# A two-layer decoder on one Trainium2 core: tokens loaded a second time turned, the key layout on GpSimd, and the border between the layers written out by hand

## The chip, the cores and the metric

The kernel runs on one core of one Trainium2 chip. The metric is the device time of one execution in microseconds; a kernel's time is the median of its runs. One further execution is recorded by the profiler, and all views come from that one. The engines are TensorE (PE, with its weight loads as PEld), VectorE (DVE), ScalarE (ACT), GpSimd (POOL) and SyncE (SP), which only issues transfers. ACT and POOL can issue transfers too. Every engine works through its own queue of instructions strictly in order.

## The reference, cut to what matters

Sixteen sequences of 256 tokens with 128 features each go through two post-norm decoder layers. Everything is float32.

```python
# layer 0
x1 = ln(x + causal_self_attention(x, 16 heads of 8))
x2 = ln(x1 + cross_attention(x1, ctx, 8 heads of 16))      # ctx: 64 rows per sequence
g  = softmax(x2 @ gate_w.T)                                  # 64 experts, the best 6 per token,
y  = sum over 6 of g_e * w2_e @ (silu(w1_e x2) * (w3_e x2))  # 64 slots per expert
x3 = ln(x2 + y + shared_expert(x2))
# layer 1
x4 = ln(x3 + causal_self_attention(x3, 16 heads of 64))
x5 = ln(x4 + cross_attention(x4, ctx, 16 heads of 64))
out = ln(2 * x5 + width_limited_self_attention(ln(x5)))
```

## The kernel before, in words

The host lays out inputs (transposes only) and launches one program. Its work falls into three stages.

**Layer 0** (lines 654 to 925). The program `contexts` (768) and sixteen programs `layer0(b)` (798), one per sequence, are recorded engine by engine and then interleaved: the string `ORDER0` names, letter by letter, whose next unit on which engine comes next. So the order on PE, DVE, ACT and POOL is that of the string (`manual_schedule`), and SP's is the scheduler's. `layer0(b)` loads 256 tokens `x` (801), turns them on PE with an identity matrix and copies the result to `xT` on DVE (803), multiplies by the query and key weights into one PSUM bank `qk` (808), and takes from it the scaled queries `qT` on DVE (810) and the keys laid out four times, each masked to a quarter of the heads (`kx`, 812: `expanded`, two copies on DVE and two on ACT, each 128x256). Then come the values, the scores (`s_0a`), softmax (`nm_0a`, `p_0a`), the turned probabilities (`ptp_0a`, `pT_0a`), the outputs, cross attention (`kx0x` is its key layout, on POOL, 839), and the gate. The gate picks six experts per token (`chosen`), counts earlier tokens per expert with a running sum `run` (889 to 892, on DVE; the next sequence's `pos` matmul reads it), computes slots, and for each of twelve choices DVE computes `hit` (the weight) and POOL scatters the tokens into `xb` in memory by an indirect transfer (914). `clear_slots` (688) fills `xb` with zeros first, from SP's queue. The context program folds weights of layer 1's cross attention and writes `gd` and `hd` to memory.

**Experts** (lines 929 to 1074). The expert weights come in eight groups, four in flight. A shared expert (`shared_hidden`, `shared_out`) runs over all tokens in eight groups of 512: products `sh`, then `hs` on ACT and DVE, then the product `z`, which DVE adds to `x2`. The routed experts read `xb` (`xe`), turn it, compute `eh`, `he` and `yp`, and store `ye` to `yb`. Groups 4 to 7 of the shared expert come last.

**Layer 1** (lines 1076 to 1234). First two buffers `vaf` are zeroed on POOL (1088), and the value bias is carried through the output projection: `bv` on DVE, eight products `bv_out` on PE, added to `l1_bout` (1091 to 1097). Then sixteen programs `layer1(b)` (1099) are interleaved by `ORDER1`. Each gathers twelve rows per token pair from `yb` by indirect transfers on POOL (`ge`, 1107), combines them on DVE with the token's weights (`xr`, 1121), normalises, turns, and goes on with self attention (`qk1`, `s_1a`), `xpb_1a` on POOL (1157, which reads `l1_bout`), cross attention over `gx` and `hx` (loaded by SP from `gd` and `hd`) and the last attention. The stage is allotted memory when the experts' is given up, so SP's first `gx` load waits for the last `z` to have been computed. The experts' part, the bias and layer 1 are three separate hand-ordered stretches, and between them the scheduler may mix their instructions; the profile shows that it put batch 0's `xr` among the shared expert's last instructions on DVE.

A helper records every operation, so nearly all instructions of the profile have the line 141 (140 afterwards); they are told apart by the names of the tiles.

Of the kernel before, what the change touches and what calls it, by code (L numbers as in the profile page):

```python
# [34 lines left out]
    ',\'#\'#$#$+$(#)($()*#*))$(*)*)()*))*())*)()*(*()*#*$#*#$**($**(#*)#$%(\'\'$%()\'\')(()*()*(1*)0-#.*((*-**.-(*..(*)#*'  # L35
    '**(///%.(*-/%).(.#/)#/.+.)+/($)-\'/$%.(%\'\'-)\'-./(/./()/--.*#./)(/-)*65/($-*2#)/#/.3(-*$2%).3((442))*-33$43\'\'.4-'
    '-./-./-/.((*/-)(-/)#//+-$/)-\'/.(/2)//%\'3(34-)33*4-)2;:/4.43(-)224242)+4)7.#+3#%34#3+438404$2.0\'4-))27.4%3+8-92'
    '92.%3+8\'3-3-.22/))2+34.4-.+42/23/-47.4-842))+/4#.+4-$-.42\'./324-4-/74.9))%+89\'8+-829.98082.97)+@493-82?7.39-77'
    '.5/87359<9.29#9-.97#.03823908289237984=7$2.7.0433078748293979828497.7.038922937340$<9=79=22978<4932.9.03#9>7>0'
    '=$>%=\'>\'57<938..00=2=7>#382>#3:=#.4.08>730EA%%8<:%=B>$D=\'2\'37<<><><353>A8=7=5>=7>85><>=B9<A>873#9358>C#C%5=B97'  # L40
    'B$<C%<8\'\'=B$C7=<\'\'9<3>35<8=>77>8<85=<9=#>7>$79<>87>A3358>5>=>B:<BC<8#B>73#3>58BC$75<8C$\'9<A>8C%37\'85JAACACA8:='
    '#BBC:BCB<I=CF#CBC?AG=?C<88A%F=CG%:<HFH=#BG:G$<H%G\'\'<H=AA8>8:B=<=:A>ACAB>ABC<C=#CB8C8:<B>AC=<$C:<=\'A=>AC<<A>C=<'
    'BCFC=C%8:8\'GAGH:GGH?AF=CHB88:HG<:OAF=B<HNFF=>GDFGHK=H#HHBD<H=AHF%=?=BGAB?HGAL$?AB\'\'FKHGCFLFM=M=?BBA?CGFCGABHFF'
    'HGHAGC=HF=?BAGAHBFBC?LFHAHAKFLCHBKHGH==?HMLLMA?FBMKLDHLMBLAM=K=?BLAMBK?LLCFLMBMMFKHM=AB?TKMP#MSMKBDGMLFQKPGMDP'
    'LRQKIRKLGIQLFKBBDMGLFKGDLMFMLFGMKQHK$KMBFBDGMKHG#MDK$HFMG#MFLMK$HMPB\'BDMGR%QRD\'QFQFRKGGQHQRFBBFDK#HMRGLD$FK\'PG'
    'RLI%PG\'NPRBFBPRDGPLFQKDYGHLQKNRUGR#RX#LRQ%FGRK%KGPIGL#IQM#QRLIL%K%PMVM$KURG\'G\'ILUWWQKVIPMLPQVV$WV\'\'WQKKLPLMGPG'
    'RIQKRKPQMRPLIQKPRLPR#NRRLUGRGI$RQRIVKVPWPLKVR#LVM#GRGILWPIW$KLWPRU%GI_LQPVUQUNWUWVUWZVNVW#VSW[QSWWPLLUQW$NP$\'\''
    '%UZQW\'\'NV[P]][P^QUULRLNVQPQNURUWUVRUVWPWQZWVPLRLNWUQVPWPWQUQN[UR#WUWVPWP#RWLLNQWPUN]Q%%[S]QPUZQWLLNV[NdP[]U`Q#'
    'VcR[X]#Q]VXP%QU%QSQVZ[aS]$[\'U\'SZVZ[]U][]UV]ZZQQW`S[]VU]ZVSW]U[`WaZ]V]b[bUQZQWS[ZVaa$Sba\'\'b[UUVZVW[Z]U[]UZ[W]ZQ'
    'ZQSV]UZV]S#]]`X$]V][]QQSaUZVbZaSUa#]VaW#$]VbZbUQVSiZe]#bh#V%X[$%Z`[%\'\'Xf^a``[^b`baZb`[VZVXba#[baZXbabZ[b`$]`eb'  # L50
    '\'\'[%ZVgVeX[]#gXaZ]f`%#[a%Zf]`$[\'f\'VgVXfagZZ[`X[]a`b`abZabZ$]b`[\'\'Z`bVVX[`bebXb^ab`b[Zbf`V#bVX[fgZf#Xn[f]`$gm[`'
    'g#$Zbg[je%[^[a$`fe\'\'^eagege^fg#fgcfgac#g[[gf`#a^$g`k\'e%a^%\'`%`aejg[b[#^fkll`a%^eaeb$bf\'a\'e[[e^fgefgegf^`fg`kbe'
    'gaeg``gaea[b[^#g%`^$`ebfgj\'\'ag`kjgaglkcl[k^sealkrkl`keoag`lfaepjfblahjjljlfh`aejoaqcfqkeflckeklefloljkgklaaecf'
    'ljfgclekgpjjfkkegaajcfkelffeckjgkleplpejgljfejlaacfjlloclhlflkqepjfqjalaecpljfgpcpqfjloqkpqaacpeqfjcxooqowqokq'
    'thpmpqffhkqjqpoqkhpuqmjotkqffhpjuvvujhkotpoluvkkjolflofhpoqkqohqjppqjplkqoujqjqkokfoflhqjjohlqkjpqtqkqvmuofvfh'
    'kuuhvjoktuqvpvujoftkhplttvktrvvprjkokmpuopvmuovuvuvopvkqktmpopmtqvouqttpuuotqktkvmptuvoopvtpmutquvooqvtpvovptv'
    'kmktvuvmvvtrptovutpkokmupmqpwuwokkptmmutrutpprrtuvtuuvtpvprurtvuttuuvpprttrvutuwpprutrutuvuptprurwpurwuuwwuuuu'
    'uuwuuwwwwwww'
)
ORDER1 = (  # L60
    '&\'&$&$&&$&$$&$+,#$#+$)#%&#%+#$%$#$%)#%+#%#%#%$+$#%$$#$#)%+#$)#$$%)010$%$&.%+$#$&)%($&#)%$$(&%$%)+%($$&*$$&)#*('
    '%0.(*#*(%%0(%(*(*$$*)&(*))#&)*6)#)%0.(%#0($)#;.5*##%#$5%#$%(.%$$%($&$%)%&$%)&#$*)&3*#0))#+#.%#))%-+%.(%0%*53#*'
    '5(%#*)-$+$(/&-).*)+(/$-*)&#$*(5))#*))**$#*+$%+-/$%-&/$-/$&#/%$(5(*))..#*.(%.+.%$%+#$&)3-&$.#/:3#%-%3#/.5:-$-/3'
    '-.&8-/:($.)(&()*5($*(&*82*:)#)$*-)*)*3+*).+#)./($+/+..(%0(..*(*(0*2*3:#*$2/3(8/:-*..4480(0-.-/)-)&/-/2.3/2+..0'
    '/2)/..(042)/3(3/.30)44(4)*2)*#)4)-$/-$%2$%$2)%2%2.303/-34844:#.8#$#%$#%#$%2$$%73%-8%%%.--./-/-/#/.#.70%./.70/$'
    '8/-8/.09#.#/$0$#%#%#%-%--/-/#//#92%$3#3-4$+43+32+4335(43(&*5$2*(33\'@*5)*/5-)4+)32+.(.42*0(42:7.*3534(843?34-47'
    ')47.389+-39809)5-.+57)/.+795(.7/9)079.(.90-(?)/-2*)/.2/4?(4./)2)*)0*)-?3*.8*87.8(=08?()(*()*()*7)?*7)=*--*8(*='
    '*2=9//3(2*3242)4=24-?433534(3425.4+43=((43(*5)()*2*52*24<024=(4.470.08(<8*9)-=<.=9-88:-.92.8/8:>(842)9:+<>83:3'
    '<>)57=>,E03=58778D92793792988:3929D934<34<>D3<>3<><3>57>88578=9=:-=98=9:-../:./.7D././.--./D-./-8/B22/B<D/<=/B'
    '/<4=7/B447478>29398593797885298-89:34B-2/9:7.48:9--9.D.-/8-:B/-/2/737?979759-93-A/<.5B35=-=7>.5>==<09=.?>=1J7?'  # L70
    '>=?<8<8I>2<>3A==2=>3:2>A?84A>3:CB<CBI7C8A>B7BC==8?>7I89A89AC8:AC8A:C87CI<9==<=B>B2B?>=B>23?343?43<3I434322=432'
    '42I34G7A9G799848:A484GA:4B747G<9G9CIC=<<=><G><>7>==?>2==>?8>2AD4>=<3B?=?2>233:<42>824<4<<>:2>F>8A4G:B7BFC82GCB'
    'B<DCBBD274CB3D78F98F>BGHD<GHHF==:2HA3?G5=AB?A3CACB<6NOAC=FCB<BGCD=CC<N=>HF=>FN=HF=HFHBBADHBGCGA?GCB7=C?78D89D8'
    '98AN8989877B987N9789L<<>LF9FGN9L9F97G>L>A9>H=A7ACB?9C<BC=C8?BBAA=CB<BDC<L>ADCCNB7D78>87CBL7D979<99A=AICACA?C7C'
    '=7K9F8?L=?G7GAH8?HGGF:HGGI8<HIFG;T=<IC=AHS>GGGF<BHBFHIK=HLKDGGHIFBMKGHGDHALKBILHAGLIMGMBMIKBCKSMKBMCKLMB<DMLLD'
    'F==F>S=>K=L>KQK>SL<QHHM<=SF>===<MG<=S><Q>K>ALB>>A>ABF>CQCGCFCFBHAHGDHBHAGDG<BCGGI<AQ>KCI=SLALMQM<LB<N<>=N<=>L<'
    '>PDLFL>FNBH<HHFQDHGIBMGFIFFHL<PDHQ>NHA=FHB<HF=MDHKL?RN=@YXLKKLMFMMXMKLGAGMPBKCILPRMNLGPMLIFQRPMGNLQFQRNRLQGNFG'
    'HXAGHPBPGRIPGRIPRGFXRFHAQHQHQABHXBCBCBKBCKBXCBABCAGMACAGICFBCVICPGCVCFFQCPVPMVRKHQHVFLXVKGSILKKLMKGMKMAMILALUN'
    'GCMBPMLLNMVMILQNALQKRBNBRQQASAACQQASCKCKCKMKMAMMAFUCRGBVFGMAKRBIHQWPQMDSBQKE_SQ^PLPLRPRFRPGNURQQ^ULRKRQQURLVUR'
    'QSVKVWQVNWLWSWKLSMUSLMULWNULWNUWL^UWKVKVMFVMV^MGFMGHGHGF^GHPGHGPGR^FLRPHGHLHFQNHF[KHN[HH[UHL[KKWU[MMK^V[PLXNQP'  # L80
    'PQRFLRRFZPQHNRPQSGRULRQQSR[RNQVSFQVFWFSGGFHFVVPXHHHWFFRPVVXHPWGPPKRFLZRGRNKRVLWKIZLXMPG]]V[JXd[URcVUUcVWPWaWWU'
    'cUWZWQQZ]VVZ]SVVWZXQWPV[SZQ]V[X]P[][XQPXQRcZQRZQ]UQ]SUWQSKW[cULLMLMPLPcVZM[aKM[RLKRKMLKMLKMPLLMaRZQMZMMaSUM[aR'
    ']QcUUWVSUWVUWKQaWVKVPXMWPVV`XWLUaWRVXWKKLLKWVKXMKMUMUMURPWWWUQK^WSK`MLQKbULSZNWQaSLSOi[U[]h]P[`VV`QbX[`b^V]P[['
    'XQP]^U`VQhZR[b[abaaa[Z^Z[]Uf]^]Vh]UVWZVZWh`]V]`bV`bXV`bXZ[b[[Z^[]aU]a^U[aP][f^WWQU^WQRQhRQ`VR`aRPXfWh]QPbQPRPQ'
    'RPQRZVRQXVR[UR`fRUaRPfWPZRhWQf[ZZ[]U]]]Z[[^ZV]PP]cP]QQPX[[PR^e[RV`R^R]fX[V^PaaXPbefURVgZQbaacPbaZacZQZ]XZ]aU]V'
    ']US]ecWQbZVTnmfga`]caZmak``b`mb`be[[beaab^eaabceb[fZcbae[fgZcafgfgg[^gZc[]me[]e[g`[g^`b^[Ubmf`VVWVWUVmaWfVWVUV'
    'UWUVWUVWZkeWkZWefWk]Ugk]`]mW[Wa^U`Wa]``Vb[Zbbk^ba`acZ[baeabcbZf`]acb]UaUcbVVUWUWUW`W`Zbb`[`hbUb^Uj[WeV^k[Uf^`V'
    'g^febffXghVgYsf`fhgrfeaZaegj[gffZhlfgZ[hegj[c]efgfhegagfecfklhZgfkgh[`gja]r[`[][]aer]fabjlfjbahljalckjlkkcjlkk'
    '`rklpa`ZbraZZ][Z]Z[]jr[[]j[ljk]pj]lek]p]pefegefgepgZgrfZf`h]fgfge[hpgZgfhZ[[ZgfZ]hZ]e]e]egegZbgZ`]b[gabZcea[cj'
    'ag^r[_kekll`kf`fmobjkmbkklmpjhlkjm`flkkmlkljoahljkkcolklamelomqofqkqceqkplmafecfg`jagkpmjplp`fl`ahjbaf`khfeeag'  # L90
    'oabaobaofbobpopgpeqpgqfg`qfhqqf`ah`baeb`ab`aoabopbobbep`bqjggk`jbkjljaljlelkkmlk`kljmflclk``bk`mba`abjmbj`llhl'
    '`jfbjlolahfhp`pjqahqppocqparpdelrjpfqropproqkekqqopmofoqgkeqjppmqokqrppfjqrpqkrqjklopklrkmokmkopjpqolpoqoqjljp'
    'prqqpeprqqfoqpfrlpflrokqoqkomqokqfmqoggjjqoggeplpljfrfpokreegepmgfogkgopgmpqegepqgkrpmoprqjpmoqokfqqpgjprjkrol'
    'pqkjfokeqoklkklpjlkrgljkjkljlfjklepelegfrefgkepggerlrljllojepglofkpojjqpoklkoppqpqpopqefqoopqhoqpjqfjpiqjpqqoq'
    'qoqlploolppoqoqoqjqjolkjokqpmopkrnps'
)


class Ref:


    def __init__(self, make):
        self._make, self._made = make, None
# [82 lines left out]
def kernel(ctx: ExitStack, tc: tile.TileContext, a: dict, out: bass.AP):  # L186
# [476 lines left out]
    with ExitStack() as phase_a:  # L663
# [134 lines left out]
        def layer0(b):  # L798
# [92 lines left out]
            if run_before is not None:  # L891
                nc.vector.tensor_tensor(run, run_before, run, ALU.add)
# [399 lines left out]
```

## Time and profile before

| | us |
|---|---|
| runs | 1684.14, 1684.59, 1687.62 (median 1684.59) |
| the profiled execution, its own time | 1679.19 |
| its span, first to last instruction | 1677.4 |
| mean granted TensorE clock | 0.959 |
| layer 0 ends with the first product of the shared expert | 602.21 |
| routed experts, first product | 631.54 |
| last expert store issued | 675.12 |
| layer 1, first product | 711.92 |

The page gives busy time of each engine with its share of the span; a table of 40 equal slices; queues; the chain of work that ended last, followed back from the end; and the costliest groups of instructions, with the idle time before them and what ended it. Other views answer for a stretch of time: busy time, waits, the chain, or single instructions in order. In a line of single instructions the figures are start, duration, engine, operation, output<-input and shape; the bracket holds the idle time before it and the releaser.

### The profile page before, as it was taken

To read this page: it belongs to the slowest core of one execution; us is meant where nothing else is said; L and a number is where in the kernel's file an instruction comes from. 1 tells how busy PE (TensorE), PEld (TensorE's weight loads), DVE (VectorE), ACT (ScalarE), POOL (GpSimd) and SP (SyncE) were. 2 spreads that over 40 slices of the span, in tenths; PEclk is the share of its full clock that TensorE was granted. 3 is DMA by queue.
4 is the path that set the end of the run, shared out by engine and by line. 5 is a ranking of instruction groups with operands and counts; after the bars stand their busy time and mean duration, and the time that the engine had idled before them with its cause. 6 is when DMAs were issued, how large, how long until landed. Compare 5 with 4: busy or idle time off the path is not lost.

```text
span 1677.4 us, 36931 instructions
## 1 busy us (share of the span) xinstructions
PE 1496.5 (89%) x12738; PEld 1080.5 (64%) x12738; DVE 1244.2 (74%) x3788; ACT 1108.6 (66%) x3811; POOL 830.6 (50%) x910
## 2 busy tenths in 40 slices
PE   7989988889987679688998999998999999999996
PEld 4655555556554338466776877686777677777774
DVE  5788888879887643355778878777786787788675
ACT  4776777757776312155576777677676767786766
POOL 2144445444435440456727656664564576564441
PEclk9999999989999778789999999999999999999999
DMA  4111111111100066474202233222322333220000
GB/s 142 60 41 34 60 32 33 42 48 55 47 13 1 1 172 190 52 105 48 23 14 34 40 41 44 23 36 14 48 41 31 30 43 42 36 23 4 5 1 11
DMA packets 117190, 73.89 MB, mean 44 GB/s; under 512 B 46555, under 2 KB 106808, under 8 KB 116877
## 3 DMA queue, kind: packets, MB, share of 16 engines
q1 hardware_dynamic: 104717, 58.55, 12.8%
q0 software_dynamic: 12288, 13.00, 10.6%
q8 instruction: 102, 1.67, 0.4%
q14 instruction: 83, 0.68, 0.1%
HBM read 48.05 MB, written 35.65 MB: 50 GB/s over the span
## 4 chain that ended last, share of the span: by engine, by line
PE 52%; DVE 24%; ACT 11%; issue 6%; POOL 4%; DMA 2%; another core or an unknown queue 1%; SPq 0%; POOLq 0%; DVEq 0%; ACTq 0%
PE s_1a L141 5%; PE qk L141 4%; PE o_1a L141 4%; ACT p_0a L141 4%; PE ptp_1a L141 3%; PE s_0a L141 3%; PE ptp_1f L141 3%; PE vp L141 3%; PE pj_1x L141 3%; PE pj_1a L141 2%; PE ptp_0a L141 2%; DVE nm_0a L141 2%; PE s_1x L141 2%; ACT p_1a L141 2%; DVE x L141 2%
## 5 line engine op out<-in xcount | busy, mean ns | idle before, releaser
L141 POOL DMA_INDIRECT xb<-x,slots x192 | 189.1, 985 | 263.9 <-DVE hit L141 212.6
L141 POOL TENSOR_TENSOR p_1a<-p_1a,ri_1a 128x512 f32<-128x512 f32 x192 | 197.3, 1039 | 104.5 <-DVE ri_1a L141 89.3
L141 ACT ACTIVATE p_1a<-s_1a,nm_1a 128x256 f32<-128x256 f32 (+1 forms) x512 | 210.9, 445 | 50.5 <-DVE nm_1a L141 41.7
L141 ACT ACTIVATE p_0a<-s_0a,nm_0a 128x256 f32<-128x256 f32 (+1 forms) x512 | 211.5, 451 | 35.2 <-DVE nm_0a L141 33.6
L141 POOL DMA_INDIRECT ge<-yb,slots x192 | 195.7, 1019 | 54.4 <-issue 51.9
L141 ACT COPY pT_1a<-ptp_1a 128x512 f32<-128x512 f32 x192 | 106.1, 618 | 63.1 <-PE ptp_1a L141 55.1
L141 DVE TENSOR_REDUCE nm_1a<-s_1a 128x2 f32<-128x512 f32 (+1 forms) x192 | 126.1, 673 | 21.4 <-PE s_1a L141 21.3
L141 DVE TENSOR_REDUCE nm_0a<-s_0a 128x2 f32<-128x512 f32 (+1 forms) x192 | 125.0, 682 | 11.8 <-PE s_0a L141 10.5
L141 PE MATMUL qk<-x3T,l_wqkv 128*128 128x256 f32 x512 | 126.9, 390 | 2.7 <-issue 1.4
L141 ACT ACTIVATE p_1f<-s_1f,nm_1f 128x256 f32<-128x256 f32 x256 | 119.0, 499 | 10.4 <-DVE nm_1f L141 9.3
L141 PE MATMUL ptp_0a<-ident,p_0a 128*128 128x128 f32 x768 | 112.1, 281 | 13.5 <-ACT p_0a L141 7.9
L141 ACT COPY pT_0a<-ptp_0a 128x512 f32<-128x512 f32 x192 | 106.4, 615 | 23.7 <-PE ptp_0a L141 18.6
L141 ACT ACTIVATION_READ_ACCUMULATOR p_0a<-s_0a,nm_0a 128x1 f32 x512 | 120.8, 236 | 0.0
L141 ACT ACTIVATION_READ_ACCUMULATOR p_1a<-s_1a,nm_1a 128x1 f32 x512 | 117.9, 230 | 0.0
L141 PEld LDWEIGHTS qk<-x3T,l_wqkv 128*128 128x128 f32 x512 | 95.8, 197 | 20.1 <-issue 7.7
L141 PEld LDWEIGHTS ptp_0a<-ident,p_0a 128*128 128x128 f32 x768 | 86.4, 143 | 34.0 <-ACT p_0a L141 20.6
L141 PE MATMUL ptp_1a<-ident,p_1a 128*128 128x128 f32 x768 | 101.1, 275 | 7.7 <-POOL p_1a L141 3.9
L141 PE MATMUL s_1a<-kT,qT 64*128 64x256 f32 (+1 forms) x1024 | 104.4, 342 | 3.3 <-issue 2.3
L141 POOL TENSOR_TENSOR p_1x<-p_1x,cri_1x 128x512 f32<-128x512 f32 x64 | 65.9, 1044 | 66.6 <-DVE cri_1x L141 41.9
L141 PE MATMUL o_1a<-pT_1a,v 128*64 128x128 f32 x1536 | 95.4, 276 | 3.0 <-ACT p_1a L141 1.2
L141 PEld LDWEIGHTS s_1a<-kT,qT 64*128 64x128 f32 x1024 | 81.5, 192 | 23.3 <-issue 11.4
L141 DVE SCALAR_TENSOR_TENSOR xr<-ge,slot_w,xr 128x128 f32<-128x128 f32 x160 | 61.2, 383 | 46.8 <-DMA ge<-yb,slots 42.7
(258 smaller groups left out, 3710.9 us busy)
## 6 DMA issues: line engine op xcount, KB each, us to landing
gd<-g1x_sb SPq DMA_DIRECT2D x32, 256.0 KB
hd<-h1x_sb SPq DMA_DIRECT2D x32, 256.0 KB
gx<-gd SPq DMA_DIRECT2D x16, 512.0 KB
hx<-hd SPq DMA_DIRECT2D x32, 256.0 KB
xb<-x,slots POOLq DMA_INDIRECT x192
ge<-yb,slots POOLq DMA_INDIRECT x192
e<-in_w1T SPq DMA_DIRECT2D x8, 352.0 KB
e<-in_w3T SPq DMA_DIRECT2D x8, 352.0 KB
```

The lines of the kernel that those rows point to most:

```text
L141: r = f(*[made(x) for x in a], **{n: made(x) for n, x in k.items()})
```

## The change

**Layer 0.** The host also passes the tokens transposed, and each sequence loads both forms; the turning of `x` on PE and its DVE copy are gone. The factor of the queries is multiplied once into the query weights. One copy on ACT takes queries and keys out of PSUM (`qkT`), and one POOL instruction lays out the keys (`kx`, 128x1024). The running sum moves to POOL. The first sequence's tokens and `l0_wqkvT` are loaded first, the other weights in another order; the slots are cleared from ACT's queue, ahead of ACT's first other work, instead of SP's. `fw`, a pool of small tiles, now ends with layer 0. `ORDER0` is a new string.

**Border and layer 1.** `vaf` is zeroed on DVE with other constants in `widths`, from memory allotted earlier; so is the pool `v2` of the gathers. One hand-ordered stretch now covers experts, bias and layer 1. The order at the border is written out: gathers of batch 0 after the last expert, the bias between shared groups 7 and 6, batch 0's combine behind the shared outputs. `ORDER1` differs little.

```diff
+        def tokens(b):
+            x = x0_pool.tile([P, 2, D], F32, tag="xin", bufs=3, name=f"x_{b}")
+            xT = x0_pool.tile([P, T], F32, tag="xinT", bufs=3, name=f"xT_{b}")
+            nc.sync.dma_start(xT, a["xT"][:, b * T : (b + 1) * T])
+            nc.sync.dma_start(x, a["x"][b * T : (b + 1) * T, :].rearrange("(i p) d -> p i d", p=P))
+            return x, xT
+
+        tokens0 = tokens(0)
         l0_wqkv = load("l0_wqkvT", [D, 3 * D], pool=x0_pool)
+        nc.scalar.dma_start(
+            xb.rearrange("(s p) d -> p s d", p=P),
+            zero.unsqueeze(1).to_broadcast([P, NSLOT // P, D]),
+        )
+        nc.scalar.dma_start(yb[NSLOT : NSLOT + 1, :], zero[0:1, :])
+        nc.vector.tensor_scalar(l0_wqkv[:, :D], l0_wqkv[:, :D], float(8**-0.5), None, ALU.mult)
...
-            transposed(x, xT, f"x_{b}")
+            x, xT = tokens(b) if b else tokens0
...
-            nc.vector.tensor_scalar(qT[:, 0, :], qk[:, :T], float(8**-0.5), None, ALU.mult)
+            qkT = x0_pool.tile([P, 2, T], F32, tag="qkT0", bufs=2, name=f"qkT0_{b}")
+            nc.scalar.copy(qkT.rearrange("p i t -> p (i t)"), qk)
             kx = kx_pool.tile([P, 4, T], F32, tag="kx0", name=f"kx0_{b}")
-            expanded(qk[:, T:], sm8, kx)
+            nc.gpsimd.tensor_tensor(
+                kx, qkT[:, 1, :].unsqueeze(1).to_broadcast([P, 4, T]), sm8.unsqueeze(2).to_broadcast([P, 4, T]), ALU.mult,
+            )
...
-            nc.vector.tensor_tensor(run, chosen[:, 0, :], chosen[:, 1, :], ALU.add)
+            nc.gpsimd.tensor_tensor(run, chosen[:, 0, :], chosen[:, 1, :], ALU.add)
             if run_before is not None:
-                nc.vector.tensor_tensor(run, run_before, run, ALU.add)
+                nc.gpsimd.tensor_tensor(run, run_before, run, ALU.add)
...
-    for t in vaf:
-        nc.gpsimd.memset(t, 0.0)
...
-        hs = shared_hidden(4)
-        expert_out(7, he)
-        shared(4, 8, hs)
+    hs4 = shared_hidden(4)
+    expert_out(7, he)
+    bv = value_bias()
+    gathered(0)
+    hs5 = shared_hidden(5)
+    shared_out(4, hs4)
+    hs6 = shared_hidden(6)
+    shared_out(5, hs5)
+    hs7 = shared_hidden(7)
+    add_value_bias(bv)
+    shared_out(6, hs6)
+    combine(0, (0,))
+    shared_out(7, hs7)
+    combine(0, (1,))
```

`gathered(b)` issues the twelve gathers of a batch, `combine(b, halves)` holds its `xr` instructions, and `value_bias` and `add_value_bias` hold the bias work with `bv` in two tiles of 128x512.

## The prediction

> **What bounds the kernel now.** The profiled execution took 1679.19 us (span 1677.4); the three timed runs have a median of 1684.59. I make the sum against the profiled execution and then move it by the 5.4 us between the two. First I read the page's busy times, then busy time by stretches.
>
> ```profile
> PE 1496.5 (89%) x12738; PEld 1080.5 (64%) x12738; DVE 1244.2 (74%) x3788; ACT 1108.6 (66%) x3811; POOL 830.6 (50%) x910
> ```
>
> ```profile
> 200.00:300.00 100.00, 87.42 (x800) 55.20 (x802) 86.24 (x313) 74.69 (x278) 45.70 (x50) 1.00 0.11 33
> 680.00:700.00 20.00, 10.86 (x49) 6.24 (x47) 7.84 (x21) 2.37 (x4) 10.68 (x11) 0.80 0.41 40
> 700.00:720.00 20.00, 16.38 (x62) 14.18 (x63) 8.19 (x21) 2.73 (x6) 11.61 (x12) 0.60 0.83 125
> 800.00:900.00 100.00, 96.09 (x813) 75.19 (x810) 75.54 (x206) 69.56 (x235) 56.44 (x61) 1.00 0.17 24
> ```
>
> After the stretch come PE, PEld, DVE, ACT and POOL, the granted clock, the DMA share and GB/s. Layer 0 (here 200 to 300) is held by PE and DVE together, 87 and 86 of 100. Layer 1 (800 to 900) is PE alone, 96. Between them lies the border, where PE is busy 11 of 20 us and then runs at clock 0.60. So a cheaper layer 0 counts where its instructions are on the chain, and the border has time to give back. The border by its instructions (start, duration, what ended the idle time before):
>
> ```profile
> 690.71 2.10 PE L141 MATMUL z<-ws2T,hs 88*128 88x128 f32 x14 [1.99 <-DVE xr L141]
> 699.96 0.80 PE L141 MATMUL z<-ws2T,hs 88*128 88x128 f32 x2 [7.14 <-DVE hs L141]
> 707.13 3.76 PE L141 MATMUL bv_out<-l_wout,bv 128*128 128x128 f32 x16 [1.48 <-DVE bv L141]
> 711.92 9.16 PE L141 MATMUL qk<-x3T,l_wqkv 128*128 128x256 f32 x32 [0.61 <-DVE x3T L141]
> ...
> 698.37 0.35 DVE L141 SCALAR_TENSOR_TENSOR xr<-ge,slot_w,xr 128x128 f32<-128x128 f32 x1 [0.84 <-DMA ge<-yb,slots]
> 701.05 0.60 DVE L141 TENSOR_SCALAR x<-xr,mv_0f,rs_0f 128x128 f32<-128x128 f32 x2 [0.85 <-POOL rs_0f L141]
> ...
> 674.53 0.99 POOL L141 MEMSET vaf<- 128x512 f32 x2 [53.32 <-PE yp L141]
> 678.36 1.06 POOL L141 DMA_INDIRECT ge<-yb,slots  x1 [2.84 <-issue]
> 711.29 0.72 POOL L141 TENSOR_TENSOR xpb_1a<-x,l_bout 128x256 f32<-128x256 f32 x1 [5.02 <-DVE l_bout L141]
> ```
>
> DVE takes batch 0's combine (xr) one gather at a time ahead of the shared expert's hs and x; PE waits 7.14 us for hs, then does z, bv_out and only at 711.92 layer 1's first qk, though batch 0's tokens were ready at 701.65. POOL stands 5.02 us for l_bout with batch 1's gathers queued behind.
>
> **The border, part by part.** The hoisted memset frees nothing: the 53 us wait it ends is idle POOL, and the gathers need the last expert store, issued at 675.12, so the first still starts near 678.4 and the last xr of batch 0 still near 698.4, its x at 701.65. What moves is PE's queue: bv_out and both z now stand free of the combine. From 688.3 (where PE reached z) it needs bv_out, 1.9 us at full clock and 3.76 at half, and twice about 1.95 for z: done by 694 to 697. Then transposes (0.64), copy (0.42), and qk starts near 703.0 instead of 711.92: 8.9 us. Against this stands that SP's layer-1 loads (gx, hx), released at 705.64 by the last z, start 9 us earlier too, onto the last two gathers. Those took 5.2 and 5.6 us from start to use; under these loads one issued at 721.31 was used at 733.53, 12.2 us. That bounds the cost at 6.6. Batch 1 gains as well: l_bout is done early, so the 5.02 us wait goes and its last gather starts at about 716.4; batch 0's first row maximum (733.80) stands behind it on DVE, and comes 5 to 11 us earlier. Border: -8, from -2 to -12. Splitting the bv copy in two costs 0.7 us of idle DVE.
>
> **Layer 0.** Per batch DVE loses the xT copy (0.415), the query scaling (0.421), two key expansions (2 x 0.476) and the running counts (0.183 + 0.305): 2.28 us, 36 in all; the one scaling of the weights returns 0.3. ACT loses 2 x 0.488 and gains one 128x512 copy from PSUM (pT_0a's row: 0.615): -0.36, 6 in all. PE loses two transposes, 0.38 at most: 6. POOL gains the key layout, 128x1024; its 128x512 twin kx0x takes 1.046 and 128x256 0.748, so 1.7 to 2.1, and two count additions, between DVE's 0.2 and POOL's 0.73 for its smallest rows; I take 2.0 + 1.2, 51 in all, on an engine busy 46%.
>
> How much was on the path? I followed the chain from 100 to 550 in stretches of 50 us and added its pieces: DVE 177, PE 169, ACT 78, issue 22, POOL 6. Of the removed instructions xT had 1.65, the query scaling 3.09, kx 4.93 on DVE and 1.70 on ACT, the counts 3.77, and a third of tp_x 1.2: 16.3 us over 13.6 batches, 19 over 16. That is the most to be had; behind each stands another engine nearly as late (PE 87, DVE 86), so I take half, -10. Below it, nothing; above, PE's shorter queue waits for fewer late DVE results, -22.
>
> A rule speaks against this part. The Trainium skill, "SBUF — State Buffer", section "Who interferes with whom": a DVE instruction with two SBUF inputs and a GpSimd instruction that reads SBUF exclude each other, and the second waits for the whole of the first. The trace shows it:
>
> ```profile
> 570.15 1.93 DVE L141 TENSOR_TENSOR sc<-sc,grc 128x128 f32<-128x128 f32 x1
> ...
> 570.88 1.03 POOL L141 TENSOR_TENSOR kx0x<-kT0x,hm 128x512 f32<-128x512 f32 x1
> ```
>
> sc has a median of 0.292 and ends here with POOL's kx0x. If every new key layout caught such an instruction whole, the price were 16 x 2.0 = 32 us, all of DVE's relief. But hit, the most frequent of them, has a mean of 0.295 over 177 against a median of 0.279, 2.8 us in all, and the excess of sc, sb, chosen, run and key adds some 4: about 7 us for 75 us of such POOL work. For 51 us more that makes 5 on DVE, 2 on the chain, within my half.
>
> The scores now wait for POOL's layout instead of DVE's and ACT's. Queued behind that on PE is everything of the batches in flight; ahead of it on POOL stand two to four scatters, each 0.97 + 0.3 us and waiting for its hit. In the rewritten order qk is taken ahead: from batch 4 on 38 to 115 rows of PE lie between a batch's qk and its scores (33 once), where before it was 40 to 86. I take no cost; the rival below prices it. The counts moved to POOL are read by the next batch's pos; most have a whole batch of time.
>
> **Start.** The chain of before shows SP's l0x_wk, its ninth transfer, issuing only when the first, ctxT, has landed (0.79 + 3.78, then 4.59): eight at a time.
>
> ```profile
> 4.59 0.33 SPq L141 DMA_DIRECT2D l0x_wk<-in_l0x_wk  x1
> 7.88 0.40 SPq L141 DMA_DIRECT2D xb<-zero  x1
> 8.32 5.53 SPq L141 DMA_DIRECT2D yb<-zero  x1
> ```
>
> The clear (2 MB) on ACT's queue now goes first, and SP's l0x_wq comes eight transfers after it, so it waits until the clear has landed. From 10 to 16 us before, DMA moved 301 to 347 GB/s at a share over 1, so the 3.1 MB ahead need about 9 us from 2.2: 11.5. Twelve more issues at 0.47 put batch 1's xT at 17.5, landed near 20 (an x of before took 2.4). PE's order has batch 1's qk before batch 0's scores, which so start near 21.5 (qk took 1.0 to 2.1) instead of 19.94. ACT is held by its two issues for some 6 us and then loads its table (1.28), until about 9; that hides behind the same wait. Context products left over are offset by qk and vp done ahead. Start: +2, from -3 to +8.
>
> **Between.** Expert weights are now issued after layer 1's weights, the same bytes by 624, and the tokens that the experts wait for come at 626.0 from the last scatter; that ends one scatter (1.28) sooner or not. -1, within 2. Layer 1's order changes little: 0, within 3.
>
> Sum: +2 - 10 - 1 - 8 = -17: 1662.2 for a profiled execution, 1667.6 as a median.
>
> **Rivals.** (1) Layer 0 gives nothing, since each removed instruction had another engine as late: +2 + 0 - 1 - 8 = -7, 1677.6. For it: ACT's p_0a alone is 10.7% of that chain and isn't touched. Against: 16.3 us of the chain are removed instructions. (2) Slower: POOL becomes layer 0's gate. It took 15.3 us of scatters and 4.7 of other work in some 33 us per batch; now 23.2, in strict order, and scatters waited for hits 75 times, up to 11.0 us. If the keys come late by 2 us per batch on the chain, 16 x 2 = 32, and -17 becomes +15: 1699.6. It decides from 17/16 = 1.1 us per batch. Against: POOL is 6 of 453 us of the chain, and the lead above. (3) All of the chain's share and a full border: 0 - 19 - 1 - 11 = -31, 1653.6.
>
> **Chances.** Forecast 0.52, rival 1 0.20, rival 3 0.15, rival 2 0.13. A difference under 0.2%, 3.4 us, can't be told from none. Rival 1 may end there (0.05 of its 0.20), so faster 0.82, same 0.05, slower 0.13. The range leaves out most of rival 2 and rival 3's far end: 1650 to 1683.
>
> **What would show it.** Right: the first layer-1 qk about 4.6 us after batch 0's last xr, which was 13.5 before; no DVE hs wait of 7 us on PE, POOL not waiting for l_bout; DVE in layer 0 near 80%, PE above 89%; first s_0a near 21.5. Wrong: PE waits at s_0a for POOL's kx or at pos for run; gathers slowed by gx and hx; first scores later than 25.

## The result and the profile after

The change made the kernel slower: 1708.34 us (median of 4 runs, 1703.07 to 1709.97) against 1684.37 (1679.32 to 1687.62), a ratio of 1.015 with a 95% interval of 1.0114 to 1.0185. The prediction was 1667.6. The profiled execution took 1706.71 us (span 1705.0) at a mean granted clock of 0.948; before it was 0.959.

The page's busy times, and busy time by stretches (columns as in the prediction; the border now lies at 710 to 750):

```profile
PE 1499.8 (88%) x12706; PEld 1083.7 (64%) x12706; DVE 1231.4 (72%) x3697; ACT 1105.0 (65%) x3795; POOL 869.9 (51%) x955
```

```profile
200.00:300.00 100.00, 91.76 (x751) 56.21 (x750) 82.23 (x290) 71.10 (x257) 51.00 (x56) 0.95 0.18 56
710.00:730.00 20.00, 14.63 (x79) 10.26 (x77) 8.08 (x18) 2.37 (x4) 10.40 (x11) 0.86 0.52 68
730.00:750.00 20.00, 13.10 (x42) 8.95 (x42) 6.62 (x21) 5.61 (x11) 13.63 (x14) 0.80 1.19 177
800.00:900.00 100.00, 94.91 (x761) 71.74 (x760) 75.90 (x199) 69.05 (x235) 60.44 (x63) 0.99 0.15 15
```

Two traps lie here. First, PE in layer 0 (200 to 300) is busier than before (91.76 against 87.42), yet the records hold 751 matmuls instead of 800, and its granted clock was 0.95 instead of 1.00. A busy share is not progress. Second, DVE did get lighter (1231.4 us in all against 1244.2), and nothing came of it.

Where the time went is read from milestones. Up to the shared expert's first product layer 0 took 634.23 us, before 602.21: 32.0 lost, in steps (by each sequence's first `pos` product it was 16 behind at the third sequence, 8 at the sixth, 32 at the eleventh and at the last). From the routed experts' first product to layer 1's first product it is 73.34 us, before 80.37: 7.0 won. From there to the end it is 970.1 us, before 965.5: 4.6 of that given back.

What the 32 us of layer 0 consist of on PE, from the stage before and then after:

```profile
0.00:602.21 602.21, 509.98 (x4370) 318.29 (x4371) 478.28 (x1698) 411.34 (x1522) 245.81 (x285) 0.95 0.14 43
```

```profile
0.00:634.23 634.23, 519.25 (x4338) 325.20 (x4339) 460.89 (x1609) 406.74 (x1506) 287.00 (x333) 0.92 0.15 44
```

PE stood idle for 115.0 us instead of 92.2, and it was busy 9.3 us longer although it had less to do, at a clock of 0.92 instead of 0.95. The trace records this clock as 1.0 or 0.5 and nothing between. In layer 0 it was 0.5 for 60.3 us before, in 7 stretches, and for 104.3 after, in 16. In the 3.4 us ahead of these stretches PE was busy for 47% in the mean before and 37% after, against 85% and 82% of the whole stage. So low clock follows idle PE in these traces, and a wait can be paid a second time by the products behind it. No run here sets the clock alone, so how much of the 32 us this is stays open. The same figure was 71.5 us in carried_late, 115.5 in new_late and 165.2 in tail_stretched, which come below.

The start, the first lines of each queue that matter:

```profile
3.63 1.13 SPq L140 DMA_DIRECT2D l0x_wk<-in_l0x_wk  x1
...
12.39 0.33 SPq L140 DMA_DIRECT2D l0x_wq<-in_l0x_wq  x1
...
17.87 0.43 SPq L140 DMA_DIRECT2D xT<-in_xT  x1
```

```profile
20.23 2.08 PE L140 MATMUL qk<-xT,l_wqkvT 128*128 128x256 f32 x4 [5.33 <-DMA xT<-in_xT]
22.23 2.09 PE L140 MATMUL s_0a<-kx,qkT 32*128 32x512 f32 x8
```

l0x_wq comes eight transfers behind the clear's start and waited for it (12.39); batch 1's tokens landed near 20 and PE stood 5.33 us for them; the first scores came at 22.23. That step was right.

### The profile page after: what moved, and what is told of

The parts are those of the page before. It is cut to its first block, busy times and chain, and to the rows that moved or that the text cites. A ratio compares the mean times of both kernels' runs of the same rounds, so it can differ in the third digit from the quotient of the medians.

```text
span 1705.0 us, 36862 instructions
## 1 busy us (share of the span) xinstructions
PE 1499.8 (88%) x12706; PEld 1083.7 (64%) x12706; DVE 1231.4 (72%) x3697; ACT 1105.0 (65%) x3795; POOL 869.9 (51%) x955
## 3 DMA queue, kind: packets, MB, share of 16 engines
q1 hardware_dynamic: 102907, 58.55, 12.6%
## 4 chain that ended last, share of the span: by engine, by line
PE 52%; DVE 21%; ACT 9%; issue 7%; POOL 4%; DMA 3%; another core or an unknown queue 0%; SPq 0%; POOLq 0%; DVEq 0%; ACTq 0%
PE s_1a L140 5%; PE qk L140 4%; PE o_1a L140 4%; PE s_0a L140 4%; PE ptp_1a L140 3%; PE ptp_0a L140 3%; PE ptp_1f L140 3%; PE vp L140 2%; PE pj_1x L140 2%; PE pj_1a L140 2%; ACT p_0a L140 2%; PE s_1x L140 2%; PE o_0a L140 2%; DVE nm_0a L140 2%; DVE x L140 2%
```

## The border: the first product is not the gate

After, PE at the border, from the single instructions in order:

```profile
717.96 1.95 PE L140 MATMUL bv_out<-l_wout,bv 128*128 128x128 f32 x16
719.75 3.14 PE L140 MATMUL z<-ws2T,hs 88*128 88x128 f32 x25
...
733.62 0.66 PE L140 MATMUL tp_x<-ident,x 128*128 128x128 f32 x2 [7.48 <-DVE x L140]
734.89 8.74 PE L140 MATMUL qk<-x3T,l_wqkv 128*128 128x256 f32 x32 [0.61 <-DVE x3T L140]
...
766.91 1.12 PE L140 MATMUL ptp_1a<-ident,p_1a 128*128 128x128 f32 x4 [7.20 <-POOL p_1a L140]
769.28 0.66 PE L140 MATMUL tp_x<-ident,x 128*128 128x128 f32 x2 [1.25 <-DVE x L140]
```

bv_out and z stand clear of the combine, as forecast; the 7 us wait has moved to tp_x, and a second one (7.20) stands ahead of batch 1. Batch 1's tp_x, at 769.28, is 107.7 us after the first routed product; before it was 109.3. So seven microseconds at batch 0 were 1.6 at batch 1.

**border_alone**: layer 0 as before, only the border, the earlier pools and the new layer-1 order.

```diff
-            x, xT = tokens(b) if b else tokens0
+            transposed(x, xT, f"x_{b}")
...
-            qkT = x0_pool.tile([P, 2, T], F32, tag="qkT0", bufs=2, name=f"qkT0_{b}")
+            expanded(qk[:, T:], sm8, kx)
```

The rest of layer 0, and its order string, go back in the same way. Wherever an order changes, here and below, the edit replaces the string itself, and the lines shown for it stand for the rule that made the new string.

> Layer 0 and its order as before; only the border, the earlier vaf and v2, and the new layer-1 order are taken from the change. My step for the border (-8) gives 1684.4 - 8 = 1676; the first layer-1 qk comes about 9 us earlier than in the kernel before, at about 703. If what layer 1 lost after its first qk in the changed kernel (4.6 us) belongs to the border or to the new layer-1 order, it is 1680 to 1681 instead.

Measured: 0.999 of before (0.9976 to 1.0004). First qk 73.8 us after the first routed product, batch 1's tp_x 107.7, as in the changed kernel. The border step was right about batch 0 and wrong about the time.

**gathers_ahead**: border_alone with half of batch 1's gathers ahead of batch 0's rs_0f on POOL.

```diff
     gathered(0)
+    gathered(1, 1)
...
+                two = [w3.tile([P, 4, D], F32, tag="p", bufs=P_BUFS, name=f"ge_{n}_{i}") for i in range(2)]
```

> border_alone (layer 0 as before, 0.999 of before) with the six gathers of sequence 1's first half right behind sequence 0's, into two buffers of their own, ahead of rs_0f in POOL's queue; the other six follow where the first six stood. If sequence 1's gathers are the border's gate, its tp_x comes some 7 us earlier against the first routed product (107.7 us in border_alone) and the whole is 0.994 to 0.996 of before. If PE is held by something else there, such as gx and hx: 0.998 to 1.000.

Measured: 0.997 (0.9952 to 0.9987), but not in the way expected. Batch 1's tp_x came 107.2 us after the first routed product, no earlier, and batch 0's first qk at 82.5, which is 8.7 later than in border_alone. That this cost nothing that can be told shows again that batch 0's first product is not the gate. What kept both batches is in DVE's lines:

```profile
695.36 0.68 DVE L139 TENSOR_TENSOR hs<-hs,sh 88x512 f32<-88x512 f32 x1 [0.90 <-ACT hs L139]
704.50 0.29 DVE L139 TENSOR_TENSOR l_bout<-l_bout,bv_out 128x128 f32<-128x128 f32 x1 [8.46 <-remote]
710.23 0.69 DVE L139 TENSOR_TENSOR x<-z,x 128x512 f32<-128x512 f32 x1 [5.44 <-remote]
```

DVE stood 8.46 and 5.44 us and the view names no releaser; the last recorded product of its input bv_out ends at 696.45. The same wait is 5.69 us in the changed kernel and 4.98 in border_alone. What the trace says of it is in the last section.

## Layer 0: the work against its order

Layer 0 changed in two things at once, its work and the string that orders it. Order strings can be carried over: places of dropped instructions are left out, added ones are put beside their neighbours. With the border alike, the four corners can be run. **carried_order** is the new work in the old order, **new_order_old_work** the old work in the new order (with buffers of their own for xT and the queries).

```diff
-    interleaved(rec, [contexts] + [partial(layer0, b) for b in range(B)], ORDER0)
+    interleaved(rec, [contexts] + [partial(layer0, b) for b in range(B)], OLD_ORDER0_CARRIED)
```

> All of the changed kernel's work (tokens loaded turned, keys and counts on POOL, clear on ACT's queue, new border), but the layer-0 order of before, carried over: the dropped instructions leave their places, qkT and kx stand where the query scaling stood, run right behind chosen. If the new order costs the time: layer 0 ends no later than before, shared product at 592 to 604, and 1664 to 1678 in all. If POOL's placement of keys and counts costs it: as slow as the changed kernel, shared product near 634 and 1700 or more.

> The converse: layer 0 does the work of before (turning on PE, query scaling and keys on DVE and ACT, counts on DVE, clear on SP's queue), but in the changed kernel's order, carried back, with the new border. If the new order costs the time: shared product at 630 or later, 1705 to 1720. If POOL's placement costs it: shared product near 602 and about 1676.

Measured, as ratios to before (border included; every kernel is compared with before in its own set of runs on one chip):

| | old order | new order |
|---|---|---|
| old work | 0.999 (0.9976 to 1.0004) | 1.0328 (1.030 to 1.0356) |
| new work | 1.0036 (1.0019 to 1.0053) | 1.015 (1.0114 to 1.0185) |

Both theories had a part. The new order, against the old one carried over by this rule, costs the new work 1.14% (some 19 us of 1684). And in the old order the new work, which has less for DVE and PE, loses 0.46% instead of gaining. It depends on the order too: the new order suits the old work far worse.

**What the new work costs: POOL's queue.** Seven kernels take the new work apart.

**carried_keys_counts_back** and **keys_counts_back** (new order):

```diff
-            nc.gpsimd.tensor_tensor(
-                kx, qkT[:, 1, :].unsqueeze(1).to_broadcast([P, 4, T]), sm8.unsqueeze(2).to_broadcast([P, 4, T]), ALU.mult,
-            )
+            expanded(qkT[:, 1, :], sm8, kx)
...
-            nc.gpsimd.tensor_tensor(run, chosen[:, 0, :], chosen[:, 1, :], ALU.add)
+            nc.vector.tensor_tensor(run, chosen[:, 0, :], chosen[:, 1, :], ALU.add)
```

> The carried-over order of before with the changed kernel's start, turned load, single copy and border, but keys (two copies on DVE, two on ACT, out of qkT) and counts (DVE) off POOL. carried_order stood at 1.0036 of before and border_alone at 0.999. If keys and counts in POOL's queue make that difference: 0.999 to 1.001 of before. If the start, the turned load or the shared copy make it: 1.003 to 1.004 still.

> The changed kernel with only the keys and the counts off POOL again (two key copies on DVE and two on ACT, out of qkT; both additions on DVE), all else and the order kept. If the new order costs the time: 1705 to 1720, since the relief of DVE is taken back too. If POOL's placement costs it: 1676 to 1690.

Measured: 0.9965 (0.9948 to 0.9983) and 1.0121 (1.009 to 1.0151). With keys and counts off POOL the old order gains 0.71%, 12 us. Under the new order the gain, 0.3%, is within the intervals.

**carried_late** and **new_late**: both stay on POOL, but kx, xpb and run get other places in its queue.

```diff
+            xpb = with_bias(x, l0_bout, f"0a_{b}")
             qk = psum(f"qk0_{b}")
...
+                    if (i, j) == (0, 5):
+                        nc.gpsimd.tensor_tensor(run, chosen[:, 0, :], chosen[:, 1, :], ALU.add)
```

> carried_order with POOL's keys and counts kept, but placed where POOL hardly has to wait for them: kx 0.6 of the way from qkT to the scores in the order (xpb ahead of it), run behind the sixth scatter of its sequence. If POOL's waiting for qkT (58.3 us) and chosen (45.8 us), with rs and scatters queued behind, is what carried_order lost: 0.997 to 1.000 of before, and PE waits for x less than 17.7 us in layer 0. If the work on POOL itself costs it: 1.003 to 1.004 as before.

> The changed kernel in its new order, with only POOL's queue mended as in carried_late: kx 0.6 of the way from qkT to the scores, xpb where kx stood, run with the sixth scatter. Under the old order this gained 0.6 per cent (1.0036 to 0.9974). If POOL's queue costs as much under the new order: 1.008 to 1.010 of before. If the new order's loss is elsewhere, as keys_counts_back (1.0121) suggests: 1.012 to 1.016.

Measured: 0.9974 (0.9955 to 0.9993) and 1.0094 (1.0068 to 1.0121): 0.6% back under either order, by places alone, with the same instructions on POOL. So not the work on POOL but its place was dear. How, one case of carried_order shows. POOL, DVE and PE in order of time:

```profile
485.62 0.29 POOL L140 TENSOR_TENSOR run<-chosen 128x64 bf16<-128x64 bf16 x1 [6.36 <-DVE chosen L140]
485.99 0.30 POOL L140 TENSOR_TENSOR run<-run,run 128x64 bf16<-128x64 bf16 x1
486.25 0.72 POOL L140 TENSOR_TENSOR rs_0a<-mv_0a,neg_half 128x2 f32<-128x2 f32 x1
```

```profile
483.20 0.17 DVE L140 TENSOR_SCALAR mv_0a<-mv_0a 128x2 f32<-128x2 f32 x1
...
487.01 1.32 DVE L140 TENSOR_SCALAR x<-r0a,mv_0a,rs_0a 128x128 f32<-128x128 f32 x2 [1.55 <-POOL rs_0a L140]
```

```profile
488.22 0.49 PE L140 MATMUL tp_x<-ident,x 128*128 128x128 f32 x2 [2.38 <-DVE x L140]
```

run is needed only by the next batch's pos, a batch later. It waited 6.36 us for chosen, and another batch's rs_0a, whose input was ready at 483.37, stood behind it until 486.25. DVE then waited 1.55 us for rs_0a, and PE 2.38 for x. The sums for layer 0, of carried_order and then of carried_late (wait, us in total, times, longest):

```profile
POOL kx L140 <- ACT qkT L140: 58.3, 11, 26.3
POOL run L140 <- DVE chosen L140: 45.8, 15, 8.3
```

```profile
PE tp_x L140 <- DVE x L140: 17.7, 13, 2.6
```

```profile
POOL kx L140 <- ACT qkT L140: 48.9, 3, 26.8
```

```profile
PE tp_x L140 <- DVE x L140: 13.3, 11, 3.0
```

The wait of tp_x in carried_keys_counts_back, with neither on POOL:

```profile
PE tp_x L140 <- DVE x L140: 13.4, 11, 3.0
```

So placing both late takes all 4.3 us of the excess away. DVE's wait for rs_0a went from 6.0 us to 1.2. That is at most a third of the 12 us; the rest is not traced to a wait. Nor does the changed kernel show this path clearly: DVE waited only 0.9 us for rs_0a there, and that POOL's queue costs it 0.6% rests on new_late alone. kx still waits 48.9 us, but in 3 places at the start instead of 11, and run's line is gone. No engine ever waited long for kx or run themselves (PE for kx: 1.2 us in carried_order); those behind them paid.

**carried_counts_back**: carried_order with only the counts back on DVE.

```diff
-            nc.gpsimd.tensor_tensor(run, chosen[:, 0, :], chosen[:, 1, :], ALU.add)
+            nc.vector.tensor_tensor(run, chosen[:, 0, :], chosen[:, 1, :], ALU.add)
```

> carried_order (1.0036) with only the counts back on DVE, keys still on POOL right behind qkT. POOL's waits there were 58.3 us for qkT (kx) and 45.8 for chosen (run). If run holds the scatters and rs up: 0.998 to 1.000 of before. If kx does: 1.003. If both alike: 1.000 to 1.001.

Measured: 1.0015 (0.9994 to 1.0035): between the two, so the counts carry about 0.2% and the keys 0.5%, the split being no sharper than its intervals. tp_x waits 12.6 us here, so what the keys cost is not in that line; by which wait they cost it stays open.

**carried_old_start**: carried_order with ctxT and weights first and the clear on SP's queue, as before.

```diff
-        nc.scalar.dma_start(
+            nc.sync.dma_start(
                 xb.rearrange("(s p) d -> p s d", p=P),
```

> carried_order with the start of before: ctxT and weights first in their old order, tokens after them, the clear on SP's queue. My start step (+2) and the first s_0a (22.0 against 19.6 in border_alone) give 2.4 us: 1.0022 of before instead of 1.0036. If the start costs nothing in the end: 1.0036. If it holds most of the loss: below 1.000.

Measured: 1.0028 (1.0014 to 1.0043), 0.08% below carried_order, 1.3 us: in keeping with the forecast 2, and not to be told from none.

**turned_only**: border_alone and xT loaded, so that two transposes and a copy go.

```diff
-            transposed(x, xT, f"x_{b}")
+            nc.sync.dma_start(xT, a["xT"][:, b * T : (b + 1) * T])
```

> Layer 0, its start and order as before, with the new border, and one part of the change alone: xT is loaded, so two transposes on PE and the xT copy on DVE go. By the chain's shares (xT 1.65 and a third of tp_x 1.2 in 450 us) at most 3.4 us over 16 sequences, by my half 1.7: 0.998 of before against border_alone's 0.999. If another engine is as late everywhere: 0.999. If the second load disturbs: above 1.000.

Measured: 0.9963 (0.9946 to 0.998), against border_alone's 0.999: 4.5 us, with the two intervals from about 1 to 8. No disturbance by the loads shows.

## Layer 0: what in the order?

**new_then_old** and **old_then_new** splice the two orders near the gate of sequence 7. A unit's place is the smaller of its place in the first order and the seam, plus what its place in the second is beyond the seam, so all dependences keep their direction. The first of the two, with `a` and `b` the places in the new and the old order:

```diff
-    order = sorted(units, key=lambda u: a[u])
+    order = sorted(units, key=lambda u: min(a[u], 1330) + max(b[u] - 1330, 0))
```

> All of the changed kernel's work; layer 0's order is the new one up to about the gate of sequence 7 and from there the carried-over old one. The gate products of after and of carried_order ran within 6 us of each other up to sequence 8 and 10 to 25 us apart from sequence 9 on. If the new order loses in its second half: near carried_order's 1.0036, at most 1.007 of before. If it loses everywhere alike: about halfway to the changed kernel's 1.015, 1.009.

> The converse: the carried-over old order up to about the gate of sequence 7, then the new order. If the new order loses in its second half: 1.012 to 1.016 of before. If everywhere alike: about 1.009. If only its beginning (queries and keys of sequences 1 to 3 taken far ahead) loses: 1.003 to 1.005.

Measured: 1.0097 (1.0072 to 1.0122) and 1.0138 (1.0112 to 1.0164). Against carried_order's 1.0036 both halves lose, 0.6 and 1.0%; my reading of the gates, that only the second does, was wrong.

**copies_early**: in the new order qkT right behind its qk, va right behind vp (four qkT buffers). In the order's places (S is ACT, T is PE):

```diff
-    place[S, qkT] = its own
+    place[S, qkT] = place[T, qk] + 0.1
```

> The changed kernel in its new order, with only the copies that empty qk and vp moved: qkT stands right behind its qk in the order, the four va copies right behind vp (where the third sequence before has done with the buffer); qkT gets four buffers instead of two. In the changed kernel PE waited 24.0 us in layer 0 for something other than its inputs (a PSUM bank, by the tiles named), 9.2 in carried_order. If banks held by products that are taken ahead are what the new order loses: 1.004 to 1.009 of before, and these waits near 10. If not: 1.013 to 1.016.

Measured: 1.0279 (1.0254 to 1.0304), 1.3% slower than the changed kernel instead of faster. PE's waits other than for its inputs stayed at 25.0 us, and ACT's line in layer 0 shows the price:

```profile
ACT qkT L140 <- PE qk L140: 22.1, 11, 9.3
```

In the changed kernel this wait was 9.5 us, once. A copy right behind its product holds its engine until the product is done, and what is next on ACT queues behind it. But the run did not take away the waits that it was made to take away: they were 24.0 us in the changed kernel and 9.2 in carried_order. So it does not test the PSUM theory, and these 15 us of waits remain a candidate for what the new order loses.

**tail_stretched** and **tail_squeezed**: from the cross-attention scores to the slots, the places of each sequence are spread by 1.10 in new_late's order and squeezed by 0.87 in carried_late's.

```diff
-    place = n
+    place = first + (n - first) * factor
```

> new_late (new order, POOL's queue mended, 1.0094 of before) with one thing changed in the order: from each sequence's cross-attention scores to its slots all its places are spread by a factor 1.10, so that consumers stand further behind their producers (rT to oT 2.9 to 3.3 places in the mean, pj_0x to r0x 3.4 to 3.9 and 2.5 to 3.5). If too little room there is what the new order loses: 1.001 to 1.006 of before. If not: 1.009 or more, as each sequence also ends later.

> The converse under the old order: carried_late (0.9974 of before) with the same stretch of places squeezed by 0.87 (exp to csum 5.4 to 4.0 places, rT to oT 4.3 to 3.4, the last pj_0x to r0x 3.9 to 3.4), about the new order's distances. If room there decides: 1.004 to 1.012 of before. If not: 0.995 to 0.999.

Measured: 1.0433 (1.0406 to 1.0459) and 1.043 (1.0405 to 1.0456). More room lost 3.4%, less room 4.6%. So room in the tail gained nothing. The theory isn't excluded by this, because both edits also move the stretch among the other sequences' work. What both show is how sharp such an order is: shifting a stretch of it by about a tenth, with the work untouched, costs as much as anything else tried here or more. Which places of the new string lose its 1.2% (new_late against carried_late) stays open. That it is the string is shown: the two kernels differ in nothing else, and in both the keys and counts stand late on POOL.

**best_copy** and **best_keys_late** put together what the runs spoke for: old order and start, tokens loaded turned, one copy, counts on DVE, the border with the gathers ahead; keys on DVE and ACT in the first, late on POOL in the second. Their edits are those of carried_keys_counts_back, carried_late, carried_old_start and gathers_ahead.

> What the runs so far speak for, together: old order carried over, old start, tokens loaded turned, one copy for queries and keys, keys and counts on DVE and ACT, the new border with the gathers ahead. carried_keys_counts_back 0.9965, start 0.0008, gathers 0.004: 0.992 of before. If the gathers give nothing: 0.996.

> best_copy (0.9942 of before) with the keys on POOL again, but late as in carried_late, and the counts on DVE. carried_late against carried_keys_counts_back (0.9974 against 0.9965) says that POOL's keys give nothing even so: 0.994 to 0.996. If DVE's relief by the keys is worth something once nothing queues behind a waiting kx: 0.991 to 0.993.

Measured: 0.9942 (0.9921 to 0.9962) and 0.9921 (0.9899 to 0.9943), the second some 13 us faster than before. Between them no difference can be told; no harm by keys on POOL shows once they stand late.

## Why the prediction was wrong, step by step

The steps, with what the runs give (ratios to before, of kernels that differ in the step alone or nearly so). The forecast -10 is split by the chain's shares, where keys and counts had 10.4 of the 16.3 us:

| step | forecast | measured |
|---|---|---|
| start | +2 us | +0.08%, 1.3 us, not told from none |
| tokens loaded turned, scaling, one copy; start included | -4 +2 | 0.9990 to 0.9965: -4 us |
| keys and counts on POOL | -6 (rival 2: 32 more) | 0.9965 to 1.0036: +12 us |
| the new order | 0 | 1.0036 to 1.015: +19 us |
| border and layer 1's order | -8 and 0 | 0.999: -2 us |

The four last rows add up to +25 us; the kernel lost 24.

**The failing step is layer 0**, forecast at -8 with its start and measured at +27, and in it two terms that I set to zero. "I take no cost" for the scores' new wait priced the consumers of kx and run, and these hardly waited. The cost came on another line: strict order on POOL puts rs and the scatters, which belong to other batches, behind a kx or run that waits. I named what is queued ahead of the layout and never priced what is queued behind it. And the rewritten order entered my sum only as a lead for qk; that an order of 2500 places is itself a term, with a sign of its own, was missing. It was the largest.

**Rival 2** had the sign and the engine right and the mechanism wrong. It gave 32 us for late keys; PE waited 1.2 us for keys, POOL's share of the loss was about 12, and half of the total was not POOL at all. kx measured 1.90 us and each addition 0.30, against my 2.0 and 0.6, so the durations were good.

**The chain shares**, halved, did not overpromise for the turned load, the scaling and the copy: -2 with the start, where -4 was measured. The turned load alone gave 4.5, with an interval that reaches down to about 1, where the chain had at most 3.4. For keys and counts they promised 6 us, and none shows even when both stand late (0.9974 against 0.9965 without them on POOL).

**The lock.** The Trainium skill, "SBUF — State Buffer", "Who interferes with whom", would at its worst have given 32 us, my estimate from it; I took 5 on DVE. hit rose from a mean of 0.295 to 0.310 us over 180, 2.7 us, while sc fell from 0.482 to 0.402 and chosen from 0.364 to 0.292. But I had looked only at instructions with two inputs in SBUF, and others grew more: x<-r0a from 0.452 to 0.650 us over 32, rx_0x from 0.228 to 0.364 over 32, mv_0x from 0.186 to 0.342 over 16, some 13 us together. One case, DVE and then POOL:

```profile
331.92 1.83 DVE L140 TENSOR_SCALAR mv_0x<-mv_0x 128x2 f32<-128x2 f32 x1
```

```profile
331.84 1.89 POOL L140 TENSOR_TENSOR kx<-qkT,sm 128x1024 f32<-128x1024 f32 x1 [2.05 <-ACT qkT L140]
```

Two elements per row took as long as the whole key layout beside them. In layer 0 DVE's busy time fell by 17.4 us (478.3 to 460.9), where I had 36 less 5. So hit's row misled me too, and the step was mis-sized by some 14 us of DVE's time. Late places do not mend it: in carried_late DVE was busy 460.3 us.

**The border**: "nothing queued on PE behind the combine" held. The step failed where it took batch 0's first qk for the end of the border. The next batch needs twelve gathers in a row (712.21 to 728.32 in border_alone), and against the first routed product these started later than before (72.2 us, before 69.7): rs_0f stands ahead of them and waits for batch 0, whose combine now comes after all its gathers. I forecast batch 1's last gather 4.9 us earlier; it was 2.4.

**The signs that I set**: first layer-1 qk 4.6 us after batch 0's last xr (4.0), first s_0a near 21.5 (22.23), no 7 us hs wait, POOL not waiting for l_bout, all came true. DVE near 80% did too (82.23), and PE above 89% (91.76). These last two were poor signs, because a slower clock fills PE as well as more work does. Of the signs of being wrong, PE's waits for kx and run did not come (1.2 us and none in layer 0): they looked at the readers.

## What to carry to other kernels

Moving work to an idle engine that works in strict order is priced by what stands behind the moved instruction while it waits, and not only by its length and its readers: place it where its inputs are long there. Count also what runs beside it: here DVE kept 17 of the 36 us that were taken from it. When work and a hand-made order change together, run the four corners before explaining either. And ask of a border whether its gate is the second batch's inputs and not the first product.

## What the runs showed of the chip that was not expected

DVE's waits at the border without a named releaser were waits for PE. In the traces each of them ends within 0.07 us of an update of the semaphore that PE's products raise: at 704.48 and 710.20 in gathers_ahead, 725.16 in the changed kernel, 704.08 in border_alone. The update at 704.48, on which bv_out's addition waited, came 8.0 us behind the end that the view gives for bv_out's last product (696.45). PE's own line falters there, with pauses that end for no recorded reason:

```profile
696.28 3.06 PE L139 MATMUL z<-ws2T,hs 88*128 88x128 f32 x24
700.26 0.27 PE L139 MATMUL z<-ws2T,hs 88*128 88x128 f32 x1 [0.91 <-issue]
...
703.07 1.09 PE L139 MATMUL z<-ws2T,hs 88*128 88x128 f32 x3 [1.06 <-issue]
705.21 0.37 PE L139 MATMUL z<-ws2T,hs 88*128 88x128 f32 x1 [1.05 <-issue]
```

This falls in time with the gathers. In gathers_ahead, the queues from 684 to 700 us and from 700 to 706 (packets, MB, share of 16 DMA engines):

```profile
q0 software_dynamic: 304, 0.66, 36.7%
q8 instruction: 1, 0.02, 0.3%
```

```profile
q0 software_dynamic: 96, 0.20, 85.5%
```

The gathers' queue held the DMA engines 85.5% of these 6 us for 0.20 MB. The Trainium skill, "Runtime: NRT & Kernel Launch", "Instruction fetch mechanics", says that an engine fetches its instructions in 16 KiB blocks over a DMA queue, mostly hidden; the one packet of 0.02 MB on the instruction queue is of that size. A block that comes late behind the gathers would be one cause, but this trace does not show it: that packet ran from 692.49 to 693.39, ahead of the pauses, and neither instruction queue has another before 728. Why PE paused stays open.

The kernel before, unchanged, had medians from 1657 to 1694 us between sets of runs, each on one chip: 2%, more than most effects of this study. Only ratios within a set could tell them.
